# Dilation in blocks of 32 rows on four packed graphs, its step on GpSimd, and other moves between engines in a four-layer graph network

## The chip, the cores and the metric

The kernel runs on one core of a Trainium2 chip. A core has a matrix engine (TensorE, PE in the profile, with its weight loads as PEld), a vector engine (VectorE, DVE), an engine for activations (ScalarE, ACT), a general one (GpSimd, POOL), and SyncE (SP), which only issues transfers here. Each works through its own queue of instructions in order; semaphores make one wait for another. The metric is the device time of one execution in microseconds (us). Three runs of the kernel before gave 9721.92, 9722.24 and 9728.73 us; the median is 9722.24.

## The reference

The input is x of 16 graphs with 1024 nodes and 128 features, a 0/1 adjacency of 1024 x 1024 for each graph, and a node mask (all true). Four layers follow one another; each adds its output to x and normalises the sum over the features.

```python
# layer 0: attention with the adjacency as mask
scores = jnp.einsum('bih,bjh->bij', q, k)          # q, k, v = relu(x W + b)
h = jnp.clip(scores * mask, 0.0, CLAMP_HI) - NEG_PENALTY * (1.0 - mask)
out = jnp.einsum('bij,bjh->bih', jax.nn.softmax(h, axis=2), v)
# layer 1: maximum over the neighbours
pre = p[:, :, None, :] + q[:, None, :, :] + b
out = jnp.max(jax.nn.relu(pre) * adj[..., None], axis=2)
# layer 2 (GIN): sum over the neighbours, then two dense layers
# layer 3: three rounds of neighbour means on a dilated adjacency, batch norms, a dense layer
def step(carry, n):                                 # for each row n of one graph, in order
    row = jnp.take(carry, n, axis=0)
    nbi = row.astype(jnp.int32)
    num = jnp.sum(nbi)
    sf = jnp.where(num > T_DIL, (num + K_DIL - 1) // K_DIL, 1)
    rank = jnp.cumsum(nbi)
    rm = row & (rank % sf == 0)
    rm = jnp.where((mask_b[n] != 0) & (num > 1), rm, False)
    carry = carry.at[n].set(row & ~rm)
    carry = carry.at[:, n].set(carry[:, n] & ~rm)
    return (carry, None)
```

The dilation (`step`) needs only the adjacency, not the results of layers 0 to 2, but its rows are serial: what row n removes is also taken out of column n, which later rows read.

## The kernel before

The program first runs `layers_012` for all graphs, with the dilation woven in, and then the last layer in four passes over the graphs (`l` = 0 to 3).

For each graph, `max_conv` (layer 1) goes through 147 groups of seven source nodes. For a group, seven maxima on VectorE (L270, one set for 21 groups) build the maxima over all subsets of the group, three transposes (L277) and a copy on ScalarE turn three groups into tables, a product with `lit` (L284) and an activation (L286) make a one-hot code of each target's subset, a product with the table (`look_up`, L150) fetches the maximum, and VectorE folds it into `best` (L262). This is called a look-up below. Two result buffers of TensorE's memory serve the wide products. After each group `between(g)` lets other work advance: pieces of the dilation at an even rate (here 1400 pieces over 16 x 147 groups), the GIN layer of the graph before for g below 30, then the load of the next graph's adjacency rows `An` and its attention, one tile of 128 rows at every tenth group.

Before the attention's softmax (L219 to L229), GpSimd makes `off` = 1 - adjacency, TensorE adds a bf16 product of `off` with the penalty to the negated scores, and VectorE clips and takes the extreme in one pass. `layernorm` (L153 to L172) takes its statistics on VectorE and does everything else on GpSimd.

`dilation` works in 8 blocks of 128 rows, all graphs at once. `E` holds the block's rows with rows on partitions; what earlier blocks removed comes back from DRAM through `rp`, is transposed and masked off (L354), and ScalarE counts the rows outside the block. Then the 128 x 128 diagonal square `Dg`, with one graph on each of 16 partitions, is gone through row by row: ten VectorE instructions a row (L374 to L387), which find rank, number, step width and the hits, and take the hits out of column n of `Dg`. The square goes back to `E` through DRAM (`own`), and with the final counts a scan (L413) over each graph's rows gives what is removed.

The queues' order is fixed when the program is built: a scheduler sets each engine's instructions one after the other by its own model of durations, taking the order in which the program emits them as priority. On the chip each engine then follows its queue.

## Time and profile before

| what | value |
|---|---|
| median of three runs | 9722.24 us |
| the profiled execution | 9721.92 us, span 9720.1 us |
| mean granted clock of TensorE | 0.932 |
| TensorE busy | 8365.7 us (86%) |
| VectorE busy | 7624.2 us (78%), 16197 instructions |
| ScalarE busy | 4286.9 us (44%) |
| GpSimd busy | 1095.8 us (11%), 1423 instructions |
| first product with a table | at 137.2 us |
| layers 0 to 2 with the dilation, to the last layer norm | until about 7887 us |
| last layer, three rounds | 7887 to about 9560 us |
| last layer, final pass | 9560 to 9720.1 us |

A line of the timeline has the start in us, the duration, the engine, the line of the kernel, the operation, its tiles (out<-in) with partitions x elements, and in brackets the idle time before it with what ended it; lines of one kind in a row are merged (x4). A line of a table of stretches has the stretch, its length, the busy time of TensorE, of its weight loads, of VectorE, ScalarE and GpSimd, each with the number of instructions, then the granted clock, the share of the transfer engines and GB/s. Matrix products are pipelined and their ends modelled, so TensorE's pace is read from the starts.

### The profile page before, as it was taken

The page shows a single profiled execution, that of the slowest core. Times are in us where ns is not written, and L with a number is a line of the kernel's source. Part 1 is how long each engine was busy: PE and PEld are TensorE (multiplying, and loading weights), DVE is VectorE, ACT ScalarE, POOL GpSimd, SP SyncE. Part 2 cuts the span into 40 slices and gives each one's busy share as a digit, 9 for nine tenths or more (in the row PEclk, how much of TensorE's full clock was granted, in tenths as well). Part 3 has the DMA queues.
Part 4 walks back from the last instruction along what each step waited for, and adds up shares of the span by engine and source line. Part 5 has one row for each costly group of instructions (what it writes and reads, how often), then busy time and mean ns, then how long its engine had stood idle before and what let it go on. Part 6 is the DMA issues. An engine that isn't in the chain of part 4 may idle for free. (4 is left out here: it accounts for less than half of the span.)

```text
span 9720.1 us, 86636 instructions
## 1 busy us (share of the span) xinstructions
PE 8365.7 (86%) x29288; PEld 4084.1 (42%) x29288; DVE 7624.2 (78%) x16197; ACT 4286.9 (44%) x5170; POOL 1095.8 (11%) x1423
## 2 busy tenths in 40 slices
PE   7989898999899989898989898989898967778774
PEld 4444444444444444444444444444444433334333
DVE  4998599869886988699859986998699958845454
ACT  3445544554465445444554455445544621122221
POOL 1010101010101010101010101010101010101116
PEclk8999999999999999999999999999999978889886
DMA  3010201020102010201020102010200057733332
GB/s 47 1 22 19 35 1 22 19 37 1 22 20 39 1 22 20 40 1 22 19 43 1 22 18 46 1 22 18 47 1 11 11 159 201 200 115 130 130 130 75
DMA packets 317237, 435.20 MB, mean 45 GB/s; under 512 B 105445, under 2 KB 156792, under 8 KB 316662
## 3 DMA queue, kind: packets, MB, share of 16 engines
q1 hardware_dynamic: 219696, 295.75, 9.2%
q0 software_dynamic: 92560, 132.72, 8.8%
q8 instruction: 230, 3.77, 0.2%
q10 hardware_dynamic: 4534, 1.19, 0.1%
q14 instruction: 217, 1.78, 0.1%
HBM read 461.64 MB, written 119.54 MB: 60 GB/s over the span
## 5 line engine op out<-in xcount | busy, mean ns | idle before, releaser
L150 PE MATMUL pg<-hot,table 128*128 128x512 f32 x9408 | 4548.7, 605 | 134.4 <-DVE best L262 42.8
L286 ACT ACTIVATE hot<-pm,one_less 128x1024 f32<-128x1024 f32 x2352 | 2617.1, 1113 | 2235.1 <-PE pm L284 2080.4
L262 DVE TENSOR_TENSOR best<-best,pg 128x1024 f32<-128x1024 f32 x2336 | 2828.8, 1211 | 534.5 <-PE pg L150 530.4
L150 PEld LDWEIGHTS pg<-hot,table 128*128 128x128 f32 x9408 | 1729.4, 191 | 1770.3 <-issue 1137.5
L284 PE MATMUL pm<-AT,lit 126*128 126x512 bf16 x4704 | 1437.2, 385 | 190.9 <-ACT hot L286 101.3
L284 PEld LDWEIGHTS <-lit 126*128 126x128 bf16 x4704 | 461.0, 99 | 1099.8 <-issue 1067.1
L279 ACT COPY table<-pt 128x384 f32<-128x384 f32 x784 | 373.3, 477 | 816.5 <-PE pt L277 811.5
L219 POOL TENSOR_SCALAR off<-An 128x1024 bf16<-128x1024 bf16 x128 | 164.2, 1283 | 3578.7 <-PE psc L223 3183.0
L277 PE MATMUL pt<-ident,sub 128*128 128x128 f32 x2352 | 410.8, 283 | 178.3 <-DVE sub L270 88.6
L189 PE MATMUL pagg<-m,part 128*128 128x512 bf16 x2304 | 529.0, 382 | 34.9 <-DVE inv L530 25.4
L277 PEld LDWEIGHTS pt<-ident,sub 128*128 128x128 f32 x2352 | 304.4, 146 | 516.6 <-issue 270.2
L374 DVE TENSOR_TENSOR_SCAN rank<-Dg,before 16x128 f32<-16x128 uint8 x1016 | 498.4, 491 | 27.2
L270 DVE TENSOR_TENSOR sub<-sub,q 128x21 f32<-128x21 f32 (+6 forms) x784 | 434.9, 555 | 49.3 <-ACT q L252 43.9
L387 DVE TENSOR_TENSOR Dg<-Dg,hit 16x127 uint8<-16x127 uint8 (+63 forms) x1016 | 454.2, 447 | 24.5
L189 PEld LDWEIGHTS <-part 128*128 128x128 bf16 x3072 | 298.2, 98 | 394.9 <-issue 53.4
L385 DVE SCALAR_TENSOR_TENSOR hit<-rank,sc,hit 16x128 f32<-16x128 f32 x1016 | 348.1, 343 | 25.6
L557 PE MATMUL pl<-w_L_gnn_Wl,hT 128*128 128x128 f32 x768 | 199.1, 367 | 178.6 <-ACT hT L581 113.2
L178 ACT CAST part<-left 128x1024 bf16<-128x1024 f32 x128 | 133.7, 1044 | 482.9 <-DVE left L180 482.8
L384 DVE TENSOR_SCALAR hit<-rank,sc 16x128 f32<-16x128 f32 x1016 | 342.7, 337 | 0.0
L532 DVE RECIPROCAL inv<-inv 128x1024 f32<-128x1024 f32 x48 | 314.3, 6548 | 19.3 <-ACT inv L531 19.3
L560 DVE SCALAR_TENSOR_TENSOR x<-pl,nm,x 128x128 f32<-128x128 f32 x384 | 129.5, 337 | 252.2 <-PE pl L557 161.4
L171 POOL TENSOR_SCALAR X<-y,ln_mv 128x128 f32<-128x128 f32 x384 | 319.4, 848 | 5.2
(172 smaller groups left out, 8512.2 us busy)
## 6 DMA issues: line engine op xcount, KB each, us to landing
m<-kept SPq DMA_DIRECT2D x32, 2048.0 KB, 9.4
An<-in_adj_dram POOLq DMA_DIRECT2D x16, 2048.0 KB, 14.3
removed<-gone SPq DMA_DIRECT2D x128, 256.0 KB, 2.0
m<-in_adjT_dram POOLq DMA_DIRECT2D x16, 2048.0 KB, 13.6
gone_all<-removed SPq DMA_DIRECT2D x16, 2048.0 KB, 9.7
kept<-m SPq DMA_DIRECT2D x16, 2048.0 KB, 14.2
AT<-in_adjT_dram POOLq DMA_DIRECT2D x16, 2016.0 KB, 14.6
hidden<-r SPq DMA_DIRECT2D x48, 512.0 KB, 3.8
```

The source lines that it names most:

```text
L150: nc.tensor.matmul(p[:, s], lhsT, rhs[:, s], start=True, stop=True)
L189: nc.tensor.matmul(p[:, s], parts[k][:, c, :], m[:, c, s], start=(c == 0 and k == 0), stop=(c == T - 1 and k == 2))
L262: nc.vector.tensor_max(best, best, pg)
L270: nc.vector.tensor_max(sub[:, :, n:2 * n], sub[:, :, 0:n], qg[:, g0:g0 + TG, k:k + 1].to_broadcast([P, TG, n]))
L277: nc.tensor.transpose(pt[:, k * P:(k + 1) * P], sub[:, g - g0 + k, :], ident)
L279: nc.scalar.copy(table.rearrange("s g o -> s (g o)"), pt[:, :3 * P])
L284: nc.tensor.matmul(pm[:, s], lit[:rows, r, :], AT[:rows, c, s], start=True, stop=True)
L286: nc.scalar.activation(hot, pm, AF.Relu, bias=one_less)
L374: nc.vector.tensor_tensor_scan(rank1, mine, mine, before[:, n:n + 1], op0=ALU.add, op1=ALU.max)
L384: nc.vector.tensor_scalar(hit, rank1, at, every, op0=ALU.is_equal, op1=ALU.max)
L385: nc.vector.scalar_tensor_tensor(hit, rank1, at2, hit, op0=ALU.is_equal, op1=ALU.max)
L387: nc.vector.tensor_tensor(Dg[:, n + 1:, n], Dg[:, n + 1:, n], hit[:, n + 1:], op=ALU.is_gt)
```

## The change

The dilation works in 32 blocks of 32 rows (`R`, `K`). `E` holds four graphs packed on the partitions (32 rows each), four such groups side by side, in two buffers; the next block's `E` and `Dg` are loaded while the steps of this one run, and its rows are counted there (`count_rest`), except for what the last block removed, which is masked off at the block's start. The removed entries are transposed in squares of 32 on VectorE and written to `removed_T`, from which `gone_T` reads whole rows; the transposes on TensorE go. The counts reach the one-graph-per-partition form through small products with `of_graph` and `of_row`. In the step, the scan over 32 columns stays on VectorE; the other operations are eleven on GpSimd, on the columns right of n only. There are 31 steps a block, 992 in all, in place of 1016.

Beside it: the attention's mask is applied on VectorE in three passes (minimum and product with the adjacency, sum with a penalty tile that GpSimd writes in f32, maximum) in place of the bf16 product with one pass; `layernorm` takes mean and variance with an aggregation on VectorE and does the eight products there, GpSimd keeps the power; the mask in rows (`half_rows`) is loaded by 16 small transfers. The last layer is unchanged but for `layernorm`. The removed lines of `dilation` stand in the code above.

```diff
 TG = 21
+R, G = 32, 4
+K, Q = N // R, B // G
 LOWEST = -(2.0**100)
 MAGIC = 2.0**23
 CLAMP_HI = 90000000000000.0
-PENALTY = 2.0**100
+NEG_PENALTY = 9000000000000000.0
...
+    half_rows = consts.tile([P, K, Q], F32, name="half_rows")
+    for b in range(B):
+        q, g = divmod(b, G)
+        nc.gpsimd.dma_start(out=half_rows[g * R:(g + 1) * R, :, q],
+                            in_=a["nodemask"][b].rearrange("(k r) -> r k", r=R))
+    nc.vector.tensor_scalar(half_rows, half_rows, 0.5, None, op0=ALU.mult)
+
+    of_graph = consts.tile([P, G], F32, name="of_graph")
+    nc.vector.tensor_reduce(of_graph, ident.rearrange("p (g r) -> p g r", g=G), axis=mybir.AxisListType.X, op=ALU.add)
+    of_row = consts.tile([P, R], F32, name="of_row")
+    nc.vector.tensor_reduce(of_row, ident.rearrange("p (g r) -> p r g", g=G), axis=mybir.AxisListType.X, op=ALU.add)
...
+    removed = dram.tile([B, N, N], BF, name="removed")
+    removed_T = dram.tile([K, P, Q, N], BF, name="removed_T")
...
         st = small.tile([P, T, 6], F32, name="ln_st")
+        mv = small.tile([P, T, 2], F32, name="ln_mv")
+        rs = small.tile([P, T], F32, name="ln_rs")
         for t in range(T):
             nc.vector.bn_stats(out=st[:, t, :], in_=src[:, t, :])
...
+            nc.vector.bn_aggr(out=mv[:, t, :], in_=st[:, t, :])
+        nc.gpsimd.tensor_scalar(rs, mv[:, :, 1], LN_EPS, None, op0=ALU.add)
+        nc.gpsimd.tensor_tensor(rs, rs, mhalf, op=ALU.pow)
         for t in range(T):
-            gp.tensor_scalar(dst[:, t, :], src[:, t, :], mean[:, t:t + 1], rs[:, t:t + 1],
-                             op0=ALU.subtract, op1=ALU.mult)
+            nc.vector.tensor_scalar(dst[:, t, :], src[:, t, :], mv[:, t, 0:1], rs[:, t:t + 1],
+                                    op0=ALU.subtract, op1=ALU.mult)
...
-            nc.gpsimd.tensor_scalar_mul(kT, kT, -1.0)
...
-                off = w4.tile([P, N], BF, name="off", tag="pen")
-                nc.gpsimd.tensor_scalar(off, An[:, t, :], -1.0, 1.0, op0=ALU.mult, op1=ALU.add)
-                psc = wide("psc")
-                for s in halves:
-                    nc.tensor.matmul(psc[:, s], qT[:, t * P:(t + 1) * P], kT[:, s], start=True, stop=False)
-                    nc.tensor.matmul(psc[:, s], penalty, off[:, s], start=False, stop=True)
+                psc = product(qT[:, t * P:(t + 1) * P], kT, "psc")
+                pen = w4.tile([P, N], F32, name="pen")
+                nc.gpsimd.tensor_scalar(pen, An[:, t, :], -1.0, NEG_PENALTY, op0=ALU.add, op1=ALU.mult)
                 e = w4.tile([P, N], F32, name="e", bufs=2)
 
+                nc.vector.scalar_tensor_tensor(e, psc, CLAMP_HI, An[:, t, :], op0=ALU.min, op1=ALU.mult)
+                nc.vector.tensor_add(e, e, pen)
                 top = small.tile([P, 1], F32, name="top")
-                nc.vector.tensor_scalar(e, psc, -CLAMP_HI, None, op0=ALU.max, op1=ALU.min, accum_out=top)
+                nc.vector.tensor_reduce(top, e, axis=mybir.AxisListType.X, op=ALU.max, negate=True)
                 total = small.tile([P, 1], F32, name="total")
-                nc.scalar.activation(e, e, AF.Exp, bias=top, scale=-1.0, accum_out=total)
+                nc.scalar.activation(e, e, AF.Exp, bias=top, accum_out=total)
...
         def dilation():
...
+            adj_q = adj.rearrange("(q g) n m -> g n q m", g=G)
+            removed_q = removed.rearrange("(q g) n m -> g n q m", g=G)
+
+            def load(k):
+                own = slice(k * R, (k + 1) * R)
+                E = dil.tile([P, Q, N], U8, name="E", bufs=2)
+                for g in range(G):
+                    nc.gpsimd.dma_start(out=E[g * R:(g + 1) * R], in_=adj_q[g, own])
+                Dg = dil.tile([B, R, R], BF, name="Dg", bufs=2)
                 nc.gpsimd.dma_start(out=Dg, in_=adj[:, own, own])
...
+                gone_T = None
+                if k > 1:
+                    gone_T = dil.tile([P, Q, N], BF, name="gone_T")
+                    for q in range(Q):
+                        nc.sync.dma_start(out=gone_T[:, q, :(k - 1) * R],
+                                          in_=removed_T[k, :, q, :(k - 1) * R])
+
+                counts = dil.tile([P, 4, Q], F32, name="counts", bufs=2)
+                nc.gpsimd.memset(counts, 0.0)
+                return E, Dg, gone_T, counts
+
+            def count_rest(k, E, gone_T, counts):
+
+                for q in range(Q):
+                    if k > 1:
+                        nc.vector.scalar_tensor_tensor(
+                            E[:, q, :(k - 1) * R], E[:, q, :(k - 1) * R], 1.0, gone_T[:, q, :(k - 1) * R],
+                            op0=ALU.mult, op1=ALU.is_gt, accum_out=counts[:, 0, q:q + 1])
+                    if k < K - 1:
+                        junk = dil.tile([P, N], U8, name="junk")
+                        nc.scalar.activation(junk[:, :N - (k + 1) * R], E[:, q, (k + 1) * R:], AF.Copy,
+                                             accum_out=counts[:, 1, q:q + 1])
                     yield
+
+            now, last_T = load(0), None
+            for _ in count_rest(0, now[0], now[2], now[3]):
+                pass
+            for k in range(K):
+                E, Dg, _, counts = now
+                own = slice(k * R, (k + 1) * R)
+                if k:
+                    prev = slice((k - 1) * R, k * R)
+                    nc.vector.tensor_tensor(E[:, :, prev], E[:, :, prev], last_T[:, :, 0, :], op=ALU.is_gt)
+                    nc.vector.tensor_reduce(counts[:, 2, :], E[:, :, prev], axis=mybir.AxisListType.X, op=ALU.add)
+                spread = dil.tile([P, 3, Q, G], F32, name="spread")
+                nc.vector.tensor_mul(spread, counts[:, 0:3, :].unsqueeze(3).to_broadcast([P, 3, Q, G]),
+                                     of_graph.unsqueeze(1).unsqueeze(1).to_broadcast([P, 3, Q, G]))
                 p = bank("pc")
...
+                for i, s in enumerate((0, 2, 1)):
+                    at = slice(0, R) if s != 1 else slice(R, 2 * R)
+                    nc.tensor.matmul(p[:B, at], spread[:, s].rearrange("p q g -> p (q g)"), of_row,
+                                     start=(s != 2), stop=(s != 0))
+                yield
+                around = dil.tile([B, 2, R], F32, name="around")
+                nc.vector.tensor_scalar_add(around[:, 0, :], p[:B, 0:R], 1.0)
+                nc.vector.tensor_scalar_add(around[:, 1, :], p[:B, R:2 * R], -0.5)
+                if k + 1 < K:
+                    following = load(k + 1)
+                    rest = count_rest(k + 1, following[0], following[2], following[3])
+                yield
+                for n in range(R - 1):
+                    if n % 4 == 3 and k + 1 < K:
+                        next(rest, None)
                     mine = Dg[:, n, :]
...
+                    m = slice(k * R + n, k * R + n + 1)
+                    rank1 = small.tile([B, R], F32, name="rank1")
+                    nc.vector.tensor_tensor_scan(rank1, mine, mine, around[:, 0, n:n + 1], op0=ALU.add, op1=ALU.max)
                     sc = small.tile([B, 5], F32, name="sc")
                     half, h1, at, every, at2 = (sc[:, i:i + 1] for i in range(5))
...
+                    gp = nc.gpsimd
+                    gp.tensor_scalar(half, rank1[:, R - 1:R], around[:, 1, n:n + 1], half_mask[:, m],
+                                     op0=ALU.add, op1=ALU.mult)
+                    gp.tensor_scalar(h1, half, MAGIC, 1.0 - MAGIC, op0=ALU.add, op1=ALU.add)
+                    gp.tensor_scalar(at, half, 5.5, h1, op0=ALU.is_gt, op1=ALU.mult)
+                    gp.tensor_scalar(every, half, 1.0, at, op0=ALU.is_gt, op1=ALU.is_gt)
+                    gp.tensor_scalar(at2, at, 2.0, -1.0, op0=ALU.mult, op1=ALU.add)
+                    hit = small.tile([B, 2, R], F32, name="hit")
+                    left = R - 1 - n
+                    one, two = hit[:, 0, :left], hit[:, 1, :left]
+                    gp.tensor_scalar(one, rank1[:, n + 1:], at, every, op0=ALU.is_equal, op1=ALU.max)
+                    gp.tensor_scalar(two, rank1[:, n + 1:], at2, None, op0=ALU.is_equal)
+                    gp.tensor_add(one, one, two)
+                    gp.tensor_mul(one, one, mine[:, n + 1:])
+                    gp.tensor_mul(one, one, Dg[:, n + 1:, n])
+                    gp.tensor_sub(Dg[:, n + 1:, n], Dg[:, n + 1:, n], one)
                     yield
 
...
+                Du = dil.tile([B, R, R], U8, name="Du")
+                nc.gpsimd.tensor_copy(Du, Dg)
+                Dd = dram.tile([B, R, R], U8, name=f"own{k}")
+                nc.sync.dma_start(out=Dd, in_=Du)
+                for g in range(G):
+                    nc.sync.dma_start(out=E[g * R:(g + 1) * R, :, own],
+                                      in_=Dd.rearrange("(q g) n m -> g n q m", g=G)[g])
+                yield
+                yield
+                nc.vector.tensor_reduce(counts[:, 3, :], E[:, :, own], axis=mybir.AxisListType.X, op=ALU.add)
+                num = dil.tile([P, Q], F32, name="num")
+                nc.vector.tensor_reduce(num, counts.rearrange("p s q -> p q s"), axis=mybir.AxisListType.X, op=ALU.add)
+
+                half = dil.tile([P, Q], F32, name="half")
+                nc.vector.scalar_tensor_tensor(half, num, 0.5, half_rows[:, k, :], op0=ALU.add, op1=ALU.mult)
+                sf = dil.tile([P, Q], F32, name="sf")
                 nc.vector.tensor_scalar(sf, half, MAGIC, -MAGIC, op0=ALU.add, op1=ALU.add)
...
+                scale = dil.tile([P, Q], F32, name="scale")
                 nc.vector.tensor_scalar(scale, half, 5.5, None, op0=ALU.is_gt)
                 nc.vector.tensor_mul(sf, sf, scale)
...
+                centre = dil.tile([P, Q], F32, name="centre")
                 nc.vector.tensor_scalar_mul(centre, sf, -1.5)
...
+                width = dil.tile([P, Q], F32, name="width")
                 nc.vector.tensor_scalar(width, half, 1.0, -1.0, op0=ALU.is_gt, op1=ALU.add)
                 nc.vector.scalar_tensor_tensor(width, sf, 0.5, width, op0=ALU.mult, op1=ALU.add)
...
+                gone = dil.tile([P, Q, N], BF, name="gone")
+                after = K - 1 - k
+                if after:
+                    last_T = dil.tile([P, Q, after, R], BF, name="last_T")
+                ranks = [None] * Q
+                for q in range(Q + 1):
+                    if q < Q:
+                        rank = ranks[q] = dil.tile([P, N], F32, name="rank", bufs=2)
+                        nc.vector.tensor_tensor_scan(rank, E[:, q, :], E[:, q, :], 0.0, op0=ALU.add, op1=ALU.max)
+                        nc.scalar.activation(rank, rank, AF.Abs, bias=centre[:, q:q + 1], scale=scale[:, q:q + 1])
+                    if q:
+                        nc.vector.scalar_tensor_tensor(gone[:, q - 1, :], ranks[q - 1], width[:, q - 1:q],
+                                                       E[:, q - 1, :], op0=ALU.is_equal, op1=ALU.mult)
+                        if after:
+                            nc.vector.transpose(last_T[:, q - 1].rearrange("p k r -> p (k r)"),
+                                                gone[:, q - 1, (k + 1) * R:])
+                            if after > 1:
+                                nc.sync.dma_start(out=removed_T[k + 2:, :, q - 1, own].rearrange("k p r -> p k r"),
+                                                  in_=last_T[:, q - 1, 1:, :])
                     yield
+                for g in range(G):
+                    nc.sync.dma_start(out=removed_q[g, own], in_=gone[g * R:(g + 1) * R])
+                if after:
+                    now = following
...
-        pieces, slots, done = T * (3 * B + P - 1), B * NG, 0
+        pieces, slots, done = K * (R + 8), B * NG, 0
```

## Prediction

> **What bounds the kernel now.** I read the page's busy table first, then stretches of 25 us, then single steps in the timeline. The profiled execution took 9721.92 us (span 9720.1), against a median of 9722.24, so sums made on it stand for the median.
>
> ```profile
> PE 8365.7 (86%) x29288; PEld 4084.1 (42%) x29288; DVE 7624.2 (78%) x16197; ACT 4286.9 (44%) x5170; POOL 1095.8 (11%) x1423
> ```
>
> The layers before the last one (from the first table product at 137 to the last norm at 7887 us) hold 80% of the span. Two stretches of them (columns: us; PE, weight loads, VectorE, ScalarE, GpSimd busy with counts; clock; DMA):
>
> ```profile
> 5210.00:5235.00 25.00, 22.76 (x84) 11.45 (x85) 23.92 (x64) 12.21 (x14) 0.00 (x0) 1.00 0.00 1
> ...
> 5885.00:5910.00 25.00, 25.00 (x77) 11.44 (x77) 13.29 (x12) 14.17 (x15) 0.00 (x0) 1.00 0.00 1
> ```
>
> Where the row steps of the dilation run, VectorE is full (23.92 of 25); where they don't, TensorE is full and VectorE half idle. So the bound alternates. One step costs VectorE ten small operations (timeline of VectorE; two look-ups are woven in):
>
> ```profile
> 5709.94 0.47 DVE L374 TENSOR_TENSOR_SCAN rank<-Dg,before 16x128 f32<-16x128 uint8 x1
> 5710.44 0.26 DVE L377 TENSOR_SCALAR sc<-rank,after,half_mask 16x1 f32<-16x1 f32 x1
> ...
> 5713.24 1.20 DVE L262 TENSOR_TENSOR best<-best,pg 128x1024 f32<-128x1024 f32 x1
> 5714.38 0.14 DVE L387 TENSOR_TENSOR Dg<-Dg,hit 16x1 uint8<-16x1 uint8 x1
> ```
>
> TensorE's own pace, in the second stretch: from one transpose of tables to the next are three look-ups, 5893.56 - 5886.77 = 6.79 us, so 2.26 us each.
>
> ```profile
> 5886.77 0.49 PE L277 MATMUL pt<-ident,sub 128*128 128x128 f32 x3
> 5887.10 0.60 PE L284 MATMUL pm<-AT,lit 126*128 126x512 bf16 x2
> 5887.53 1.88 PE L150 MATMUL pg<-hot,table 128*128 128x512 f32 x4
> ...
> 5893.56 0.27 PE L277 MATMUL pt<-ident,sub 128*128 128x128 f32 x1
> ```
>
> The price of a chain on GpSimd is seen in the last layer norms, which run there back to back:
>
> ```profile
> 9706.78 0.21 POOL L164 TENSOR_TENSOR ln_mv<-ln_mv 128x8 f32<-128x8 f32 x1
> 9707.08 0.20 POOL L166 TENSOR_SCALAR ln_mv<-ln_mv 128x8 f32<-128x8 f32 x1
> 9707.36 0.24 POOL L167 TENSOR_SCALAR ln_mv<-ln_mv 128x8 f32<-128x8 f32 x1
> 9707.68 0.20 POOL L168 TENSOR_TENSOR ln_mv<-ln_mv 128x8 f32<-128x8 f32 x1
> 9707.96 1.67 POOL L169 TENSOR_TENSOR ln_mv<-ln_mv,mhalf 128x8 f32<-128x8 f32 x1
> 9709.74 6.27 POOL L171 TENSOR_SCALAR y<-x,ln_mv 128x128 f32<-128x128 f32 x8
> ```
>
> Starts of dependent ones are 0.28 to 0.32 us apart, though an operation shows 0.20 to 0.24: count 0.29 each. The 128x128 form with two per-partition scalars takes 6.27 / 8 = 0.78 us.
>
> **What the Trainium skill says.** "GPSIMD Engine Reference", section 3.1: a GpSimd instruction passes two software dispatches, and elementwise work belongs on VectorE. The trace agrees: a one-column `sc` operation on VectorE is 0.14 to 0.15 us, the smallest on GpSimd 0.20, 0.29 in a chain. "Perfetto Trace Analysis", GPSIMD Engine Instruction: time such instructions by start-to-start spacing, which I do. "SBUF — State Buffer", Who interferes with whom: a VectorE operation with two SBUF inputs and a GpSimd one that reads SBUF lock each other out. Here the trace shows it: L380 took 0.82 us from 6601.91 where its median is 0.147; a GpSimd operation had begun at 6601.68 and ran 1.05, and both end at 6602.73.
>
> **The change part by part.** (1) VectorE is relieved of nine operations a step. The ten rows L374 to L387 have means that add to 2.74 us, times 127 x 8 = 1016 steps 2.8 ms. The scan, now in 31 x 32 = 992 steps, shrinks to 32 columns (0.472 at 128, 2.283 at 1024: 2.02 ns a column, so 0.28 us), 0.28 ms in all. VectorE alone would stop being a bound.
>
> (2) The nine become eleven on GpSimd in a row, each reading the one before (only `at2` is off the chain), and the next row's scan needs the last. Step time c: 11 x 0.29 = 3.2; seven per-partition scalars in `half` (2), `at`, `every`, `one` (2), `two`; elements, six operations on 15.5 columns on average, 0.2. A scalar's price isn't shown alone. From the 0.78 us form: less 0.17 start spacing of independent ones (L161 to L162, 9706.06 to 9706.22) and less 128 elements at 0.9 ns (L219, 1024 in 1.05 us) leaves 0.50 for two; at 2.5 ns (L207, 2.79 us for 1024) it leaves 0.29. I take 0.2 each, 1.4. Hand-overs 0.10 (VectorE's reciprocal ends 9424.70, GpSimd starts 9424.80) and 0.03 back (9428.00 to 9428.03), scan 0.28. Sum 5.2; I use 5.0, since half of these operations have one element and not eight. Bounds: scalars free, 3.8; all five scalar forms at the full 0.78, 6.2.
>
> (3) Where the steps stand decides. In the built program VectorE's queue has, per graph, 146 running maxima and 62 scans, and the scans are not spread: they form two trains of 31. The first holds 17 look-ups (and the GIN layer of the graph before), the second 19 (and two attention tiles); at one place eight scans follow each other. The other 110 look-ups have none. VectorE works in order, so each look-up queued behind a scan waits for GpSimd's chain, and TensorE, with two result buffers, waits for the look-up. TensorE's work in a train: 17 x 2.26 + 48 products of L189 at 0.21 + the rest of GIN, about 10 = 58 us; 19 x 2.26 + two tiles of 4.9 (psc 1.7, pe 1.09, pav 2.05) = 53 us. A train takes 31 x 5.0 = 155 us, plus 5.5 for what cuts in (the `pen` operation, 1.05 to 2.8, on GpSimd's queue, once or twice; the seven `sub` maxima, 3.9 us with two SBUF inputs, which lock GpSimd out). So 160 us, of which TensorE idles 105. GpSimd's own queue holds, inside the first train, the load of `An`, which waits for GIN's products; these are done by then, and the loads of `E` and `Dg` stand between trains.
>
> (4) Outside trains TensorE's pace holds. Its work for 16 graphs, at the pace of the full stretches: 147 look-ups x 2.26 = 332, eight attention tiles at 4.9 = 39, queries, keys and values 11, GIN 20, so 402 a graph; the first and last have less, together 6350. Less 32 trains x 55.5 leaves 4570. (The penalty products, 2 x 0.21 x 128 = 54 us, and 448 transposes of `rp`, about 40 us, are gone from it.)
>
> (5) Graph boundaries and block ends: 25 us a graph, 400. Before, from the last sum (2987) to the next table product (3016.65) TensorE idled some 20 us; the layer norm there is cut from 10 us (L161 at 2993.68 to the last L171 at 3003.66) to about 4.5. Twice a graph a block's end waits for `Du`, two transfers of about 4 us each (`own`, `E`: 3.8 and 3.9) and the rank scan, with look-ups behind: 5 each. The transfers of `gone_T` and `removed_T` (64-byte runs) hide in the 150 us between trains; if not, rival four.
>
> (6) VectorE gains two more passes over each attention tile (by the 1.21 us of L262) and the norms' products: hidden in TensorE-bound time (13.29 of 25 busy); without that cover 2 x 1.21 x 128 = 310 us. In the last pass GpSimd is the bound (16 x 10 us = 160, the end of the span); with the eight products moved to VectorE, 8 x (0.34 + 0.28 + 0.33 by L384 + about 0.15 for the new aggregation) = 8.8 us a graph, about 140.
>
> (7) Start: 16 loads of `half_rows` (1024 elements each, ahead of the first adjacency on GpSimd's queue). `Dg`'s 2048 packets took 12.0 us, so up to 96; I take 40: 177 to the first product.
>
> Sum: 177 + 4570 + 32 x (31c + 5.5) + 400 + 45 (after the last look-up) + 1810 (last layer: 9720 - 7887, less 20) = 7180 + 992c. With c = 5.0 that is 12140, rounded **12100 us**. Made for the kernel before by the same pieces, the layers come to 408 + 20 a graph for TensorE and not the measured 7750 / 16 = 484; the rest is VectorE's step time.
>
> **The rivals.** *The chain hides (faster).* The point is c = 2.56, where the sum is 9720; at c = 2.3 the time is 9460, and with trains no longer than TensorE's work in them 8780. It needs eleven dependent GpSimd operations at under 0.2 us each; for it speaks only that one-element operations aren't shown; against it, that the eight-element ones never start closer than 0.28 when dependent. Chance 4%.
> *Scalars are free*: c = 3.8, 10900 us. For it: L166, with two constants, is no dearer than a plain one. 20%.
> *Scalars cost as in the 128-column form*: c = 6.2, 13300 us. For it: 0.78 us is the only such row. 12%.
> *The sum holds but the block ends wait for transfers*: 20 us at each of 32 ends, 12700 us. Against it, the 3.8 us of `own`. 8%.
> *No change*: only if c fell by chance near 2.56. 1%. That the change doesn't do what it says I exclude; the queues show it.
>
> **How the numbers follow.** My own case (c from 4.5 to 5.6: 11600 to 12700) has 55%, and 12100 is its middle. The range for 8 in 10 reaches to the rivals on the slow side, 10700 (c = 3.6) to 13300 (c = 6.2). A measurement here tells 0.2% (the runs spread 0.07%). Faster 4%, within 0.2% 1%, slower 95%.
>
> **What would show it.** Right: a scan of 0.28 us on VectorE, preceded by idle time released by GpSimd, about 60 times a graph, in all 2 to 4 ms; GpSimd busy for some 5 ms; starts of successive scans about 5 us apart in trains of 31, with TensorE a third busy and its clock lowered there; slices of 23.9 of 25 on VectorE gone; full TensorE between trains at 2.26 us a look-up. Wrong: scans 2.5 us apart or less; VectorE still full; idle time before the counting or ranking operations released by DMA (rival four); or GpSimd idle inside trains.

## The result, and the profile after

The changed kernel takes 11832.91 us (median of four runs, 11831.25 to 11839.35); the kernel before, beside it on the same chip, took 9722.94. The ratio is 1.217, 95% interval 1.215 to 1.219. The prediction said 12100, within 10700 to 13300. The mechanism is the one predicted. The total is closer than its parts, because a term that was too large and one that was too small partly cancel.

The page of the kernel after, its busy table:

```profile
PE 8829.5 (75%) x28760; PEld 4298.2 (36%) x28760; DVE 6102.5 (52%) x8800; ACT 4116.0 (35%) x4714; POOL 3640.8 (31%) x11584
```

VectorE fell from 7624 to 6102 us and is no longer near full; TensorE is busy for 464 us more than before, on less work and at a lower clock (0.866 in place of 0.932), and its share fell from 86 to 75%. No engine is full over the run, so much of the time is in waits. One graph in four stretches, as windows (columns: from:to us; PE, weight loads, VectorE, ScalarE, GpSimd busy with counts; granted clock; DMA share; GB/s). The first and third are the two trains of 31 steps, the others lie between them:

```profile
5071.30:5199.40 128.10, 75.30 (x226) 34.06 (x226) 35.49 (x75) 23.99 (x26) 93.08 (x332) 0.80 0.09 17
5199.40:5378.80 179.40, 165.63 (x537) 81.26 (x536) 112.76 (x146) 88.47 (x104) 11.92 (x23) 0.95 0.12 21
5378.80:5503.70 124.90, 71.48 (x202) 32.87 (x200) 43.10 (x74) 30.86 (x37) 94.53 (x332) 0.81 0.00 0
5503.70:5692.60 188.90, 154.68 (x488) 75.08 (x489) 119.69 (x172) 87.90 (x103) 14.29 (x26) 0.91 0.16 26
```

In a train GpSimd works and TensorE is busy for 75 of 128 us, and slowly: the mean clock is 0.80, at which 75 us would be some 60 us of work at full clock (an estimate; the prediction counted 58). A graph is 621 us in place of 484. The slowness is seen in single look-ups of this train, one after a long idle stretch and a later one:

```profile
5118.10 3.78 PE L160 MATMUL pg<-hot,table 128*128 128x512 f32 x4 [21.77 <-DVE hT L311]
...
5124.98 1.88 PE L160 MATMUL pg<-hot,table 128*128 128x512 f32 x4
```

One step inside a train, where nothing cuts in (timeline: start us, duration us):

```profile
5092.21 0.27 DVE L403 TENSOR_TENSOR_SCAN rank<-Dg,around 16x32 f32<-16x32 bf16 x1 [3.85 <-POOL Dg L421]
5092.59 0.33 POOL L407 TENSOR_SCALAR sc<-rank,around,half_mask 16x1 f32<-16x1 f32 x1 [0.41 <-DVE rank L403]
5093.01 0.23 POOL L409 TENSOR_SCALAR sc<-sc 16x1 f32<-16x1 f32 x1
5093.34 0.30 POOL L410 TENSOR_SCALAR sc<-sc 16x1 f32<-16x1 f32 x1
...
5093.99 0.18 POOL L412 TENSOR_SCALAR sc<-sc 16x1 f32<-16x1 f32 x1
5094.16 0.47 POOL L416 TENSOR_SCALAR hit<-rank,sc 16x26 f32<-16x26 f32 x1
5094.63 0.34 POOL L417 TENSOR_SCALAR hit<-rank,sc 16x26 f32<-16x26 f32 x1
5095.05 0.23 POOL L418 TENSOR_TENSOR hit<-hit 16x26 f32<-16x26 f32 x1
...
5095.98 0.29 POOL L421 TENSOR_TENSOR Dg<-Dg,hit 16x26 bf16<-16x26 bf16 x1
5096.31 0.27 DVE L403 TENSOR_TENSOR_SCAN rank<-Dg,around 16x32 f32<-16x32 bf16 x1 [3.83 <-POOL Dg L421]
```

Scan to scan is 5096.31 - 5092.21 = 4.10 us; the median over all in-train steps is 4.02. VectorE stood idle for 3.83 of it, and the bracket names who it waited for. This step and the next two as windows, where the clock is the third column from the end:

```profile
5092.21:5096.31 4.10, 4.10 (x17) 1.86 (x15) 0.27 (x1) 1.49 (x2) 3.08 (x11) 1.00 0.01 2
5096.31:5100.41 4.10, 0.02 (x1) 0.00 (x0) 0.27 (x1) 1.21 (x2) 3.08 (x11) 0.86 0.00 0
5100.41:5104.51 4.10, 0.00 (x0) 0.00 (x0) 0.30 (x2) 0.00 (x0) 3.05 (x11) 0.50 0.00 0
```

TensorE has filled its two result buffers by the end of the first step and then does nothing. In the whole run VectorE waits for this chain for 2656 us, within the 2 to 4 ms of the prediction's signs, and TensorE waits in turn (waited for: us in total, times, longest):

```profile
DVE rank L403 <- POOL Dg L421: 2656.3, 914, 4.7
...
PE pg L160 <- DVE best L261: 959.8, 371, 13.7
PE pg L160 <- DVE hT L311: 320.4, 15, 21.8
PE pm L283 <- ACT hot L285: 188.7, 176, 4.2
PE pe L233 <- ACT e L228: 188.6, 90, 7.5
...
PE pt L276 <- DVE y L241: 122.6, 15, 8.5
```

TensorE's first is the predicted one, a look-up held up behind scans. The second has the same reason: once a graph, in the first train, a look-up's product waits for the GIN layer's sum (`hT`), which stands behind scans in VectorE's queue, for up to 21.8 us. The other three (the one-hot codes, the transposes of the exponentials, and the transposes of a table that wait for attention's result) are in no step of the prediction; the experiments come back to them.

Added up like the prediction's sum (a train from its first scan to GpSimd's last subtraction):

| term | predicted | measured | difference |
|---|---|---|---|
| start, to the first table product | 177 | 102.9 | -74 |
| 32 trains | 5136 (160.5 each) | 4146 (129.6 each) | -990 |
| outside the trains, to the last look-up | 4970 | 5693 | +723 |
| after the last look-up | 1855 | 1896 | +41 |
| profiled execution | 12138 | 11837.5 | -300 |

### The profile page after: what moved, and what is told of

The parts are those of the page before. It is cut to its first block, busy times and chain, and to the rows that moved or that the text cites. A ratio compares the mean times of both kernels' runs of the same rounds, so it can differ in the third digit from the quotient of the medians.

```text
span 11837.5 us, 89809 instructions
## 1 busy us (share of the span) xinstructions
PE 8829.5 (75%) x28760; PEld 4298.2 (36%) x28760; DVE 6102.5 (52%) x8800; ACT 4116.0 (35%) x4714; POOL 3640.8 (31%) x11584
## 5 line engine op out<-in xcount | busy, mean ns | idle before, releaser
L160 PE MATMUL pg<-hot,table 128*128 128x512 f32 x9408 | 4817.9, 638 | 1313.9 <-DVE best L261 959.8
L160 PEld LDWEIGHTS pg<-hot,table 128*128 128x128 f32 x9408 | 1837.4, 203 | 3108.2 <-issue 1320.7
L283 PE MATMUL pm<-AT,lit 126*128 126x512 bf16 x4704 | 1486.6, 397 | 286.6 <-ACT hot L285 188.7
L403 DVE TENSOR_TENSOR_SCAN rank<-Dg,around 16x32 f32<-16x32 bf16 x992 | 286.3, 289 | 2656.4 <-POOL Dg L421 2656.3
L220 POOL TENSOR_SCALAR pen<-An 128x1024 f32<-128x1024 bf16 x128 | 134.4, 1050 | 2150.2 <-DVE e L224 2117.2
L407 POOL TENSOR_SCALAR sc<-rank,around,half_mask 16x1 f32<-16x1 f32 x992 | 381.8, 385 | 1159.1 <-DVE rank L403 1097.5
L588 POOL TENSOR_TENSOR inv<-inv,mask 128x1024 f32<-128x1024 f32 x48 | 135.7, 2828 | 1372.5 <-DVE inv L585 1350.5
L416 POOL TENSOR_SCALAR hit<-rank,sc 16x31 f32<-16x31 f32 (+30 forms) x992 | 443.4, 447 | 0.0
L160 PE MATMUL psc<-kT,qT 128*128 128x512 f32 x512 | 282.9, 679 | 106.8 <-DVE best L261 105.9
L417 POOL TENSOR_SCALAR hit<-rank,sc 16x31 f32<-16x31 f32 (+30 forms) x992 | 340.5, 343 | 0.0
L411 POOL TENSOR_SCALAR sc<-sc 16x1 f32<-16x1 f32 x992 | 303.1, 306 | 97.7
```

Of the source, the lines that this page charges most:

```text
L160: nc.tensor.matmul(p[:, s], lhsT, rhs[:, s], start=True, stop=True)
L283: nc.tensor.matmul(pm[:, s], lit[:rows, r, :], AT[:rows, c, s], start=True, stop=True)
L407: gp.tensor_scalar(half, rank1[:, R - 1:R], around[:, 1, n:n + 1], half_mask[:, m], op0=ALU.add, op1=ALU.mult)
L411: gp.tensor_scalar(every, half, 1.0, at, op0=ALU.is_gt, op1=ALU.is_gt)
L416: gp.tensor_scalar(one, rank1[:, n + 1:], at, every, op0=ALU.is_equal, op1=ALU.max)
L417: gp.tensor_scalar(two, rank1[:, n + 1:], at2, None, op0=ALU.is_equal)
```

## The experiments

Theory: in the bunched order of VectorE's queue, GpSimd's chain runs with too little of TensorE's work beside it. Rivals: the blocks of 32 rows cost by themselves; the chain costs wherever it stands; attention's extra passes or the norms do it. All times are medians of four runs; ratios are to the kernel before on the same chip. The experiments ran on several chips, on which the medians of the kernel before lie between 9722.81 and 9733.69 us, so a difference below some 20 us between two of them tells nothing unless they shared a chip.

**e1: the step back on VectorE.** Engine of the eleven operations only:

```diff
-                    gp = nc.gpsimd
+                    gp = nc.vector
```

> The eleven operations of a step go back to VectorE, one by one the same; the blocks of 32 rows, the attention and the norms stay as in the changed kernel. My theory (the loss is GpSimd's dependent chain, at 4.1 us a step, waited for in VectorE's queue): a step becomes some 2.2 us of VectorE's own time (eleven operations at 0.15 to 0.18 and a scan of 0.28), VectorE's work is about 440 us a graph against TensorE's 402, and the time falls to 9300 - 9800 us. Rival (the blocks of 32 rows with their 32 block ends cost by themselves): it stays above 10500. Rival (VectorE full again, worse than before because a step has eleven operations and attention two passes more): 10000 - 10500.

Measured: 9686.16 us, ratio 0.996 (0.995 to 0.998). The whole loss is gone, so the move to GpSimd together with the order that the scheduler gave it is the cause, and the 32-row blocks, which stay here, bring no loss by themselves. The same operations side by side, mean ns of one, first on VectorE here, then on GpSimd in the changed kernel (groups of instructions):

```profile
L416 DVE TENSOR_SCALAR hit<-rank,sc 16x31 f32<-16x31 f32 (+30 forms) x992 | 276.6, 279 | 0.0
...
L407 DVE TENSOR_SCALAR sc<-rank,around,half_mask 16x1 f32<-16x1 f32 x992 | 256.4, 258 | 30.0
...
L409 DVE TENSOR_SCALAR sc<-sc 16x1 f32<-16x1 f32 x992 | 138.2, 139 | 26.0
```

```profile
L416 POOL TENSOR_SCALAR hit<-rank,sc 16x31 f32<-16x31 f32 (+30 forms) x992 | 443.4, 447 | 0.0
...
L409 POOL TENSOR_SCALAR sc<-sc 16x1 f32<-16x1 f32 x992 | 226.1, 228 | 86.6
```

These two are some 1.6 times as long on GpSimd. But the order changed too: with the step on VectorE the scheduler sets 31 scans over 46 and 54 look-ups, in the changed kernel over 17 and 19. So e1 alone doesn't tell the chain's length from the bunching; e2 does.

**e2: the same operations, spread.** An edge of order, without a wait, ties each scan and each look-up on VectorE's queue to the one written ahead of it:

```diff
+        queued = [None]
+
+        def in_turn(ins):
+            if queued[0] is not None:
+                tc.add_manual_dep(ins.ins, queued[0].name,
+                                  mybir.DependencyInfo(mybir.DependencyClass.NoSync, mybir.DependencyReason.DATA),
+                                  reason="in_turn")
+            queued[0] = ins.ins
...
-                    nc.vector.tensor_max(best, best, pg)
+                    in_turn(nc.vector.tensor_max(best, best, pg))
...
-                    nc.vector.tensor_tensor_scan(rank1, mine, mine, around[:, 0, n:n + 1], op0=ALU.add, op1=ALU.max)
+                    in_turn(nc.vector.tensor_tensor_scan(rank1, mine, mine, around[:, 0, n:n + 1], op0=ALU.add, op1=ALU.max))
```

> The operations are the changed kernel's, on the same engines; only the order on VectorE's queue is pinned: scans and look-ups stand there in the order in which they are written, one scan to two or three look-ups (31 scans over some 60 look-ups, where the changed kernel has 31 scans over 17 to 19). My theory (it is the bunching: a look-up waits for a chain that runs with nothing of TensorE's beside it): 1.84 look-ups of 2.26 us are 4.16 us, just above a step's 4.1, so that most of the 105 us lost in a train is won back, and the time falls to 9100 - 9900 us. Rival (the chain is on the path wherever it stands, 992 x 4.1 us): 11600 - 12000. Rival (the order written out makes look-ups wait for the block ends instead): 10300 - 11000.

Measured: 9895.17 us, ratio 1.018 (1.016 to 1.019), at the slow end of the theory's range. Of the 2110 us lost, 1938 come back with every operation still on its engine and about as long as before (GpSimd is busy for 3741 us, against 3641). The timeline of this kernel shows how:

```profile
5214.58 0.27 DVE L412 TENSOR_TENSOR_SCAN rank<-Dg,around 16x32 f32<-16x32 bf16 x1 [0.88 <-POOL Dg L430]
...
5214.78 1.18 DVE L270 TENSOR_TENSOR best<-best,pg 128x1024 f32<-128x1024 f32 x1
...
5216.78 1.22 DVE L270 TENSOR_TENSOR best<-best,pg 128x1024 f32<-128x1024 f32 x1 [0.82 <-PE pg L160]
...
5218.58 0.27 DVE L412 TENSOR_TENSOR_SCAN rank<-Dg,around 16x32 f32<-16x32 bf16 x1 [0.57 <-POOL Dg L430]
```

This step still takes 4.00 us (5214.58 to 5218.58), but two look-ups pass inside it, and VectorE waits 0.57 us for GpSimd, not 3.83. The 320 us that look-ups waited for `hT` are gone from TensorE's list of waits. A train's 31 scans now stand over 55 look-ups, and the median step over all trains is 4.31 us. In a window of 36 us TensorE is busy for 35.98 and GpSimd for 26.53 beside it:

```profile
5210.00:5246.00 36.00, 35.98 (x116) 17.24 (x114) 23.63 (x32) 20.16 (x22) 26.53 (x92) 1.00 0.00 1
```

**e3: a shorter chain, bunched.** Three of the eleven operations are left out, so that part of the dilation is missing:

```diff
-                    gp.tensor_scalar(two, rank1[:, n + 1:], at2, None, op0=ALU.is_equal)
-                    gp.tensor_add(one, one, two)
-                    gp.tensor_mul(one, one, mine[:, n + 1:])
```

> Three of the eleven GpSimd operations of a step are left out (the second comparison, the sum with the first, and the product with the row), so that the wrong edges are removed: part of the dilation is missing. Their starts lie 0.42 + 0.30 + 0.30 = 1.02 us apart in the trace. My theory (every step is on the path, since a train is all chain): 992 x 1.02 = 1010 us less, 10820 us, +- 120. Rival (trains are partly bound by what else VectorE or TensorE does): less than half of that, above 11350.

Measured: 11206.30 us, 627 less than the changed kernel: neither the 1010 of the theory nor the rival's less than half. By the scan starts in the trace the step fell from 4.02 to 3.11 us, 0.91 and not 1.02, and a train from 126.1 to 97.7 us between its first and last scan: 28.4 us, over 30 steps 0.95 each on average (means over the 30 trains between the first and the last one). So inside trains the slope is complete, 32 x 28.4 = 909 us. But with shorter steps the scheduler put only 13 and 18 look-ups into the trains in place of 17 and 19. The stretches between trains grew, and the remaining 909 - 627 = 282 us are given back there. Five look-ups a graph at 2.26 us are 11.3, times 16 some 181 of these (an estimate); the other 100 I can't place.

**e9: the same shorter chain, spread.** The edits of e2 and e3 together.

> The pinned order (9895 us) with the same three GpSimd operations left out as before, so part of the dilation is missing again; the step's chain is 3.1 us in place of 4.0. My theory (spread, a step's chain hides behind its 1.84 look-ups of 4.16 us, just so): most of the slope is gone, 0 to 250 us less than 9895: 9650 - 9890. Rival (the chain is on the path wherever it stands): 0.91 x 992 = 900 less, 8990.

Measured: 9774.96 us, 120 less than e2. The same cut of 0.9 us a step is worth 909 us inside bunched trains and 120 where the steps are spread. The chain of 4 us is nearly off the path there.

**e4: the attention of before.** The penalty product on TensorE and one pass on VectorE (L219 to L229 of the kernel before) in place of the three passes:

```diff
...
-                psc = product(qT[:, t * P:(t + 1) * P], kT, "psc")
-                pen = w4.tile([P, N], F32, name="pen")
-                nc.gpsimd.tensor_scalar(pen, An[:, t, :], -1.0, NEG_PENALTY, op0=ALU.add, op1=ALU.mult)
+                off = w4.tile([P, N], BF, name="off", tag="pen")
+                nc.gpsimd.tensor_scalar(off, An[:, t, :], -1.0, 1.0, op0=ALU.mult, op1=ALU.add)
+                psc = wide("psc")
+                for s in halves:
+                    nc.tensor.matmul(psc[:, s], qT[:, t * P:(t + 1) * P], kT[:, s], start=True, stop=False)
+                    nc.tensor.matmul(psc[:, s], penalty, off[:, s], start=False, stop=True)
...
-                nc.vector.scalar_tensor_tensor(e, psc, CLAMP_HI, An[:, t, :], op0=ALU.min, op1=ALU.mult)
-                nc.vector.tensor_add(e, e, pen)
...
-                nc.vector.tensor_reduce(top, e, axis=mybir.AxisListType.X, op=ALU.max, negate=True)
+                nc.vector.tensor_scalar(e, psc, -CLAMP_HI, None, op0=ALU.max, op1=ALU.min, accum_out=top)
...
```

> The attention of the kernel before is put back (penalty product on TensorE, one pass over the scores on VectorE in place of three); all else is the changed kernel's. Step six of the prediction (the two extra passes are hidden): TensorE gets its 128 penalty products back, 54 us, so 11850 - 11920 us. Rival (VectorE is the bound for 30 - 40 us after each train, and at a graph's end, and the passes lie there): 100 - 300 us less, 11530 - 11730.

Measured: 11494.34 us, 339 less: the step of the prediction that hid the passes is wrong, and the 54 us of penalty products that TensorE has again don't outweigh it. Trains keep their length; the stretches between them lose 20 us a graph. That is what two passes of 1.21 us on eight tiles add up to (19.4), so VectorE's load seemed the cause.

**e7: spread, with the old attention.** The edits of e2 and e4 together, to see the passes where VectorE has room.

> The step stays on GpSimd with the pinned order, and attention is the kernel before's: what the move to GpSimd is worth when its two companions are taken away. My theory (VectorE is free in 4.5 of 12 us beside the spread steps, full only at the block ends): the passes are mostly hidden, a third of the 338 us that the old attention won in the bunched order: 9750 - 9900 us. Rival (they lie on the path here too): 9550 - 9650, faster than the kernel before.

Measured: 9565.70 us, ratio 0.984 (0.982 to 0.985), 329 less than e2: the rival's number. The gain is the same as in the bunched order although VectorE is busy for only 62% of e2, which spoke against its load as the reason. The waits of TensorE in the changed kernel pointed to another one: 189 us at the transposes for the exponentials, and 123 us at a table's transposes for attention's last result (`y`), which frees the bank (a smaller result buffer of TensorE) that they need. Three passes make the way from scores to exponentials 2.4 us longer, and by the trace TensorE has one to three look-ups queued between the two.

**e10: the same passes, transposes written later.** Attention keeps its three passes; only the place of the transposes, and of what follows them in a tile, moves:

```diff
                 nc.scalar.activation(e, e, AF.Exp, bias=top, accum_out=total)
+                yield
...
-                    elif g % 10 == 0:
+                    elif g % 5 == 0:
```

> The changed kernel with its own attention of three passes; only the order is changed: the transposes of the exponentials are written four or five look-ups behind the scores, where the changed kernel has one to three between. VectorE does the same work. My new theory (the two extra passes cost not by VectorE's load but by latency: TensorE's queue waits at the transposes for the exponentials and for the bank that the last product frees, 189 + 123 us in its waits): most of the 338 us that the old attention won comes back, 11500 - 11650 us. Rival (VectorE's load is the cost): above 11750.

Measured: 11492.78 us, 340 less: the whole gain of e4, with VectorE doing the same work as in the changed kernel (6109.5 us busy against 6102.5). Three to five look-ups now stand between scores and transposes. The waits of TensorE in this kernel:

```profile
PE pg L160 <- DVE best L262: 977.6, 387, 9.5
...
PE pm L284 <- ACT hot L286: 116.5, 119, 3.4
...
PE pe L234 <- ACT e L228: 5.9, 14, 0.4
```

The wait for the exponentials fell from 189 to 6 us, that for the bank is gone from the list, and that for the one-hot codes lost 72 (a wait for the table maxima, L270, grew from 146 to 236); the look-ups' wait behind scans stayed, and a train is as long as before (125.9 us from its first to its last scan in both). So the price was latency in TensorE's queue. The Trainium skill, "PSUM — Partial Sum Buffer", section Engine vs sequencer instructions, says that products start and complete in program order; the trace agrees: TensorE sits out up to 7.5 us at these transposes, and hardly any with more look-ups queued ahead of them.

**e11: spread, with later transposes.** The edits of e2 and e10: the changed kernel's own operations, all on their engines, in another order.

> The pinned order with the later transposes, attention with three passes, steps on GpSimd: the changed kernel's own operations, all of them, in another order. My theory (both losses are of order): 9560 - 9680 us, near the pinned order with the old attention (9566), and faster than the kernel before. Rival (VectorE's load): 9800 - 9900.

Measured: 9619.59 us, ratio 0.988 (0.986 to 0.990): 1.2% faster than the kernel before.

```profile
PE 8237.3 (86%) x28657; PEld 4109.6 (43%) x28760; DVE 6093.2 (64%) x8800; ACT 4110.8 (43%) x4714; POOL 3817.6 (40%) x11584
```

The counts of VectorE, ScalarE and GpSimd are those of the changed kernel, and their busy times nearly so (GpSimd's is 5% longer); the 2213 us that the changed kernel takes more come from the order alone.

**e8: the norms of before.** Statistics on VectorE, all else on GpSimd again.

```diff
-            nc.vector.bn_aggr(out=mv[:, t, :], in_=st[:, t, :])
...
-            nc.vector.tensor_scalar(dst[:, t, :], src[:, t, :], mv[:, t, 0:1], rs[:, t:t + 1],
-                                    op0=ALU.subtract, op1=ALU.mult)
+            gp.tensor_scalar(dst[:, t, :], src[:, t, :], mean[:, t:t + 1], rs[:, t:t + 1],
+                             op0=ALU.subtract, op1=ALU.mult)
```

> Only the layer norms are the kernel before's again: eight GpSimd products of 0.78 us each, and no aggregation on VectorE. By the prediction the norm at a graph's end is cut from 10 to 4.5 us on the path, so that this kernel takes 16 x 5.5 = 90 us more in the graphs and, by its step for the last pass, 20 us more there: 11940 us. Since the last pass was cut by 2.6 us only, I now expect 3 there and 90 in the graphs: 11900 - 11950. Rival (the norm at the boundary waits behind other work anyway, and VectorE is relieved of 16 small operations): within 30 us of 11833.

Measured: 11848.71 us, 16 more, no more than a measurement can tell (the rival). From a graph's last sum to the next table product the traces have 29.8 us before, 25.7 in the changed kernel, 28.7 here (medians over 15 boundaries): 3.0 us a graph, 45 in all, of which no more than 16 are seen in the time. The two longest waits there are not the norm's: TensorE waits for the transfer of `AT` and for the table maxima, 5.86 and 6.26 us in the changed kernel (below), and 5.67 and 6.26 us at the boundary of the kernel before that the prediction reads (2987 to 3016.65 us). This is a boundary in the changed kernel, as a timeline:

```profile
5662.33 1.22 DVE L291 TENSOR_TENSOR best<-best,pp 128x1024 f32<-128x1024 f32 x1 [0.50 <-PE pp L160]
...
5671.74 1.01 PE L283 MATMUL pm<-AT,lit 126*128 126x512 bf16 x2 [5.86 <-DMA AT<-in_adjT_dram]
...
5686.58 0.90 PE L276 MATMUL pt<-ident,sub 128*128 128x128 f32 x3 [6.26 <-DVE sub L269]
```

**e5 and e6: a version that beats both.** Blocks of 32 rows and the new norms stay; the step is the nine VectorE operations of the kernel before, in 32 columns, and attention is the kernel before's, as in e4. e6 has the pinned order of e2 besides.

```diff
...
-                    gp.tensor_scalar(one, rank1[:, n + 1:], at, every, op0=ALU.is_equal, op1=ALU.max)
-                    gp.tensor_scalar(two, rank1[:, n + 1:], at2, None, op0=ALU.is_equal)
-                    gp.tensor_add(one, one, two)
...
+                    nc.vector.tensor_scalar(hit, rank1, at, every, op0=ALU.is_equal, op1=ALU.max)
+                    nc.vector.scalar_tensor_tensor(hit, rank1, at2, hit, op0=ALU.is_equal, op1=ALU.max)
+                    nc.vector.tensor_mul(hit, hit, mine)
+                    nc.vector.tensor_tensor(Dg[:, n + 1:, n], Dg[:, n + 1:, n], hit[:, n + 1:], op=ALU.is_gt)
```

> The step's nine operations of the kernel before on VectorE, in 32 columns, and the attention of the kernel before; the blocks of 32 rows and the new norms stay. My theory (with the eleven operations on VectorE the kernel took 9686 us, and VectorE was full beside the steps, 11.4 of 12 us): two operations less a step (some 0.25 us x 62 = 16 us a graph) and two passes less in each attention tile (19 us) take VectorE below TensorE's 402 us of work a graph, so that 20 to 30 us a graph come off: 9150 - 9400 us, faster than both kernels. Rival (it is no longer VectorE's load but the order on its queue and the graph boundaries that cost): 9500 - 9690.

> As the one with nine operations on VectorE and the old attention, with the order of scans and look-ups pinned as written. My theory: a step and its 1.84 look-ups are 1.84 x 1.21 + 1.4 = 3.6 us of VectorE against 4.16 of TensorE, so TensorE's pace holds in the steps, and what remains is some 35 us at the graph boundary and the tails of the blocks: 440 - 455 us a graph, 9050 - 9300 us, as fast as or faster than without the pinned order. Rival (steps on VectorE need no spreading, the pinned order only takes freedom away): slower than without it by 50 - 200 us.

Measured: e5 9412.53 us, ratio 0.968 (0.966 to 0.969); e6 9438.14, ratio 0.970 (0.969 to 0.972). Both are faster than either kernel, and both are slower than the theory's ranges (9150 to 9400, 9050 to 9300). A graph takes about 471 us in either, against the 402 of TensorE's work that the prediction counted: the load on VectorE was not all that was left. The pinned order costs 26 us where steps are on VectorE (both ran on one chip, and their runs don't overlap). With equal attention, order and blocks, the step in eleven operations on GpSimd (e7, 9566) costs 128 us more than in nine on VectorE (e6): even where most of it hides, the move brought nothing.

## Why the prediction was right and wrong

**Step 1, VectorE relieved: right.** The scan took 0.27 to 0.29 us (0.28 predicted), and VectorE's full stretches in the steps are gone.

**Step 2, the chain: right in kind, its scalar term mis-sized.** I used 5.0 us; the trace has 4.0 to 4.1. Dependent starts of plain operations are 0.30 to 0.33 us apart (0.29 assumed), and the way from L421's start over the scan to the next L407 is 0.33 + 0.38 us. What failed is "I take 0.2 each, 1.4" for the per-partition scalars. In the timeline above the form with two constants spaces 0.33 us and the one with two scalars 0.42 (L407); with 26 columns two scalars space 0.47 and one 0.42, against 0.31 for a plain operation (L418). That is 0.05 to 0.11 for one, 0.36 for these five, where I had put 1.0. In the 0.78 us of the 128-column form, from which I took the price, the columns were put too low, at 0.9 to 2.5 ns each: in this trace the two-scalar form (L416) has a median of 0.40 us with one column and 0.52 with 31, some 4 ns a column, so that 128 columns alone are about 0.5 us (an estimate). Two operations also overlap their neighbours. `at2` starts only 0.17 us ahead of the next, and `two` (L417) doesn't read `one`, though the prediction has every operation but `at2` read the one before.

**Step 3, bunched trains: right, and the cause.** 31 steps a train, 17 and 19 look-ups in it, TensorE idle behind its two buffers: all as written. A train is 129.6 us, 31 x 4.02 and 5 for what cuts in (5.5 predicted). e2 and e9 show that the bunching decides, and not the chain's length by itself. Three of the signs missed in size: GpSimd is busy for 3641 us and not 5 ms, TensorE in a train for 59% (75.30 of 128.10 us) and not a third, since the low clock stretches its work, and between trains it isn't full (165.63 of 179.40).

**Steps 4 and 5, outside the trains: too small by 723 us.** Some 340 of this is attention's latency (e4, e10). The boundary was cut by 4.1 us (5.5 predicted), but the norm's part was worth 16 us in all and not 90 (e8). The rest, about 380 us or 12 for each of 32 trains, I read from the trace only. After a train VectorE is full with look-ups and the block's tail, and further on TensorE's clock is low; windows of 12 us in the changed kernel:

```profile
5223.40:5235.40 12.00, 10.63 (x34) 4.86 (x32) 11.67 (x10) 8.74 (x11) 0.00 (x0) 1.00 0.26 33
...
5259.40:5271.40 12.00, 11.98 (x40) 7.52 (x40) 2.96 (x6) 2.72 (x3) 0.00 (x0) 0.80 0.01 1
```

But the sign of rival four, idle time of VectorE that a transfer ends ahead of the counting, stands in this trace too, and TensorE waits behind it:

```profile
5250.59 0.72 DVE L362 SCALAR_TENSOR_TENSOR E<-E,gone_T 128x544 uint8<-128x544 uint8 x1 [3.90 <-DMA E<-in_adj_dram]
...
5514.26 0.29 DVE L433 TENSOR_REDUCE counts<-E 128x4 f32<-128x128 uint8 x1 [3.98 <-DMA E<-own]
...
5517.99 2.75 PE L160 MATMUL psc<-kT,qT 128*128 128x512 f32 x4 [4.35 <-DVE best L261]
```

Over the whole run these two waits of VectorE are 63.3 and 70.6 us, some 4 us a block and not the 20 of the rival. Step 5 had 5 us a block for `own`, but nothing for `E`. I ran no kernel without a block's tail or without these transfers, so the split of the 380 us stays open.

**Step 6, two more passes hidden: wrong.** The cover that I named, VectorE busy for 13 of 25 us, is an average. TensorE waits for the end of the passes, and I had counted no work queued ahead of the transposes. The price that I gave for lost cover (310 us) is close to the 339 measured, but by luck: it priced VectorE's load, and e10 shows that the latency costs. The last pass came to 157.5 us and not 140. The norm's products left GpSimd, but in the chain that ended last they stand in turn with GpSimd's power, 1.7 us, on whose end they wait; my 8.8 us a graph had only VectorE's operations (start us, duration us; shorter pieces between left out):

```profile
11695.44 1.69 POOL ln_rs L171
11697.15 2.14 DVE y L173 x8
...
11708.30 1.68 POOL ln_rs L171
11710.00 2.14 DVE y L173 x8
```

**Step 7, the start: wrong in sign.** The 16 loads of `half_rows` were done by 27.8 us, beside the first attention, and TensorE's list of waits has none for them; the first table product came at 102.9 us and not at 177. The kernel before needs 137.2; what shortened it I didn't test.

**The rivals.** The chain came near "scalars are free" (3.8 us, for which the prediction's formula gives 10950 and not the 10900 written there). With 4.02 us a step it gives 7180 + 992 x 4.02 = 11170, 670 short of the profile: a better chain alone would have made a worse forecast, and 12100 came close by luck, because steps 2 and 7 on the one side and 4 to 6 on the other erred against each other. For "the chain hides" I set a step time (2.56 us) as the point that decides. The runs put it elsewhere: at 4.0 us a step the chain nearly hides if about two look-ups stand beside each step (e2), and at 3.1 it doesn't if there are only 13 or 18 for 31 steps (e3).

## What to carry to other kernels

When a serial chain moves to another engine, look in the built queues at what stands between its links on the engine that waits: the same instructions were 2110 us slower than the kernel before when bunched, 172 when spread, and 114 faster when attention's transposes were moved back as well. Price an added operation twice, as load on its engine and as latency to whoever waits in order behind it; an engine that is half idle hides the first, only other work queued ahead of the waiting instruction hides the second. An edge of order without a semaphore won back here what the scheduler's order had lost; where the step stands on VectorE, the same edges cost 26 us (e5, e6).

## What the runs showed of the hardware

Small GpSimd operations are less far from VectorE's than I had assumed: 228 against 139 ns for one column with two constants, 447 against 279 with two scalars and 1 to 31 columns. A per-partition scalar adds 0.05 to 0.11 us on GpSimd, and about 0.06 on VectorE (258 against 139 ns for two).

The clock falls quickly: 1.00, 0.86 and 0.50 in three successive stretches of 4.1 us, of which the last two had almost no product. The Trainium skill, "TensorE: Matmul & The Clock Gate", Part 1: The HAM clock gate, says that the idle state is half rate, entered after an idle window of about 3.4 us; the 0.50 in the third stretch agrees. So idle time of TensorE is dearer than its length, since the products after it run slowly as well: the look-up after 21.77 us of idling took 3.78 us, a later one 1.88.
